# Zero products for TensorE at the heads of stages, and layer 1's head and first convolution sums moved earlier, in a four-layer graph network

## The chip, the cores and the metric

One core of a Trainium2 chip runs the whole network in one launch. The metric is device time in microseconds (us). A core has five engines, each with its own instruction queue worked in order: PE (matmuls; PEld is its weight load), DVE (vector), ACT (scalar), POOL (GpSimd, which here adds tiles and issues gathers), and SP (SyncE, which issues the other transfers). [...]

## The reference, cut

Eight batches of 2048 nodes with 64 features pass four layers; each is `x = x + layer(relu(layernorm(x)))`. `adj` is 2048x2048, sparse, and denser in its first rows.

```python
# layer 0
h = x @ W;  s = leaky_relu(h @ a_node, 0.2)
logits = where(H.T > 0, s[:, None, :], NEG)
agg = einsum('ben,bnf->bef', softmax(logits), h)          # to 64 hyperedges
industry = (adj / deg) @ (x @ W_ind)
g = ...                                                   # back to the nodes, over their hyperedges
pair = stack([industry, g]);  scores = tanh(pair @ fcW + fcb) @ av
out = einsum('bnk,bnkf->bnf', softmax(scores), pair)      # "mixing"
# layer 1: Chebyshev graph convolution, K = 3, 16 node-wise embeddings
As = [I, adj, 2 * adj @ adj - I]
x_g = einsum('knm,bmc->bnkc', As, x)
w = einsum('nd,dkio->nkio', embedding, weight)
out = einsum('bnki,nkio->bno', x_g, w) + embedding @ bias
# layer 2: three times
effects = adj @ v;  v = relu(cat(v, effects) @ W1.T + b1) @ W2.T + b2
# layer 3: attention over the edges of adj
```

## The kernel before, in words

**Tiles.** The batches are handled in four pairs q (`NP`): two batches of 64 features are the 128 partitions. Nodes are in 16 tiles of 128 (`NT`) and 4 chunks of 512 (`NC`, 4 tiles each, `TC`). "By feature" tiles have features on partitions; "by node" tiles have 128 nodes on partitions and 4x128 columns.

**Products with adj.** The adjacency is kept as lists. The first three row tiles (`HUBS`) are dense and multiplied whole; of the rest, each target tile t gets `LISTED[t]` items of 128 neighbour rows (0, 7, 6, 5, 4, ... 3; tile 0 takes 13 whole tiles). `Feed` does one such product: `dense` (L2650 on) makes 6 hub products into the bank `acc`; `listed` (L2660 on) takes item after item. For each item POOL issues a gather of 128 rows (L2613), ACT rounds it to `part_hi` (L2630), DVE subtracts to `part_lo` (L2631), and PE multiplies both by the item's 128x128 weights, cast from `cells` by ACT (L2589). Six gathers are in flight at most. Gathers read node rows from a DRAM tensor `sent`, so they wait until all 16 tiles of it are written.

**Layer 0.** `aggregate` (L896 on): per chunk the node scores (`to_pair_rows`, 4 products to 32 rows each), then per pair and chunk a broadcast of two rows of scores to 128 partitions by a product with a 32-row slice of `from_rows` (L266, L939), which DVE clips by a mask (L940). `Lists.prepare` (L2414 on) makes the lists; `x_ind` its products; `adj_product` (L310) the dense one with adj. Then `mix` (L695): for 16 (chunk, pair) steps PE makes tanh products and score products, ACT the tanh, DVE and POOL the sums; after a chunk `norm_parts` (L275), the layernorm for layer 1, is spread over the next chunk's steps. After the last chunk it runs alone: squares, a reciprocal on DVE (L291), four broadcasts and eight products on DVE (L710). The callback `each` (L881 on) gathers and turns `h` for one chunk ahead. Beside it `lists.fill` (L2507) gathers the 60 item blocks of adj and stores them as bf16.

**Layer 1** (`layer1_near`, L1640 on). Its head: `lists.load` (L2541) loads three dense row blocks through one buffer, with a DVE cast after each (L2547), and the rows for tile 0; then for 16 tiles 8 transposes of 64x64 (L1665), two copies, and a send to `sent[0]` on SP (L1667). Then the first product (16 targets, `acc` in three banks); after each target its result is sent to `sent[1]` (L1690) and turned by feature (`turn`, L1675 to 1679). Then `convolution_near`: it loads the convolution's weights and embeddings (L1708 on, L1794), makes the second product for one chunk (`product(0)`), and then walks four chunks (order 1, 0, 2, 3), in each four pairs, in each eight weight blocks taken two at a time with both batch halves, so four banks: 4 products by `w01` (128 rows), a step of the next chunk's second product, 4 products by `w2` (64 rows), and for each bank `y = (pk + bias) * emb` on DVE (L1852) and a sum on POOL (L1858) or, for the last block, on DVE.

**Layer 2** (`layer2_near`) runs three `Feed` products, then `Scores` (chunk by chunk, the layernorm for layer 3 and its score products, `pw`). **Layer 3** follows.

**What sets the order.** The program's own order fixes each engine's queue, but the framework may put independent instructions of one engine ahead of those that would wait; in the profile some of the embeddings' loads (from 639.79) and six of the first `w01` products (735.61) are ahead of their place in the text. Buffers are pools with a fixed number of tiles (`bufs`); a tile's next writer waits for the readers of the last. Every matmul goes through `mm` (L176), so groups of them are told by tile names.

## Time and profile before

| | us |
|---|---|
| median of 3 runs (lowest, highest) | 2005.93 (2004.48, 2013.83) |
| profiled execution: its own time, its span | 2004.73, 2003.0 |
| layernorm, features, checks | 0 to 103 |
| aggregation and hyperedge keys | 103 to 186 |
| lists and x_ind | 186 to 211 |
| product with adj | 211 to 449 |
| mixing | 449 to 594 |
| layer 1's head and first product | 594 to 720 |
| second product, first chunk | 720 to 765 |
| convolution | 765 to 1240 |
| layer 2 and scores | 1240 to 1700 |
| layer 3 | 1700 to 2003 |

Of 2003.0 us PE is busy 1712.0, DVE 1393.1, POOL 1036.1 and ACT 811.0. A row of the page or the timeline reads: start, time busy, engine, line, operation, the tile written and the tiles read with shape and type, how many in a row (x), and in brackets how long the engine stood idle before and what ended that. A row of windows has the stretch and its length, then for PE, PEld, DVE, ACT and POOL the busy time and the number of instructions, then the granted clock (1.00 is full), the busy share of the transfer engines and GB/s. "PEclk" on the page is the clock in tenths, 40 slices of 50 us.

### The profile page before, as it was taken

To read this page: it belongs to the slowest core of one execution; us is meant where nothing else is said; L and a number is where in the kernel's file an instruction comes from. 1 tells how busy PE (TensorE), PEld (TensorE's weight loads), DVE (VectorE), ACT (ScalarE), POOL (GpSimd) and SP (SyncE) were. 2 spreads that over 40 slices of the span, in tenths; PEclk is the share of its full clock that TensorE was granted. 3 is DMA by queue.
4 is the path that set the end of the run, shared out by engine and by line. 5 is a ranking of instruction groups with operands and counts; after the bars stand their busy time and mean duration, and the time that the engine had idled before them with its cause. 6 is when DMAs were issued, how large, how long until landed. Compare 5 with 4: busy or idle time off the path is not lost. (4 is left out here: it accounts for less than half of the span.)

```text
span 2003.0 us, 22362 instructions
## 1 busy us (share of the span) xinstructions
PE 1712.0 (85%) x7094; PEld 986.7 (49%) x7098; DVE 1393.1 (70%) x2281; ACT 811.0 (40%) x1634; POOL 1036.1 (52%) x1005
## 2 busy tenths in 40 slices
PE   6888999898977779999999998678789899378985
PEld 2446766663325544444434443567576575244432
DVE  6888788864776657676776556698787566257874
ACT  5722545445555643221110101555556553176400
POOL 1101466668734645875765453553664440657870
PEclk8888999999887979999999899889899898689997
DMA  9641223336247864232320211667687674845665
GB/s 340 260 117 44 74 95 111 106 111 202 58 135 225 242 190 123 74 116 63 85 80 32 79 48 63 214 198 253 199 261 244 184 241 136 261 117 172 172 177 193
DMA packets 125882, 305.21 MB, mean 152 GB/s; under 512 B 29345, under 2 KB 33201, under 8 KB 120241
## 3 DMA queue, kind: packets, MB, share of 16 engines
q0 software_dynamic: 45328, 149.60, 25.0%
q1 hardware_dynamic: 78112, 149.80, 22.4%
q10 hardware_dynamic: 2304, 4.20, 0.6%
q8 instruction: 60, 0.98, 0.2%
q14 instruction: 78, 0.63, 0.1%
HBM read 240.40 MB, written 63.14 MB: 152 GB/s over the span
## 5 line engine op out<-in xcount | busy, mean ns | idle before, releaser
L2613 POOL DMA_INDIRECT raw<-sent,index x300 | 315.0, 1050 | 343.0 <-DVE part_lo L2631 137.7
L2631 DVE TENSOR_TENSOR part_lo<-raw,part_hi 128x512 fp32r<-128x512 f32 x352 | 266.2, 777 | 142.9 <-ACT part_hi L2630 77.4
L2630 ACT CAST part_hi<-raw 128x512 fp32r<-128x512 f32 x352 | 212.2, 619 | 333.1 <-PE acc L176 223.5
L1858 POOL TENSOR_TENSOR half<-half,y 128x512 f32<-128x512 f32 x192 | 247.6, 1319 | 135.0 <-DVE y L1852 134.3
L176 PE MATMUL pk<-q,w 128*128 128x512 f32 (+1 forms) x768 | 301.9, 610 | 2.3 <-DVE q L1742 0.9
L176 PE MATMUL acc<-q,ident 128*128 128x512 f32 x416 | 205.9, 620 | 25.3 <-issue 12.1
L176 PE MATMUL acc<-part_hi,weights 128*128 128x512 f32 x365 | 179.3, 495 | 31.8 <-ACT part_hi L2630 17.6
L176 PE MATMUL acc<-part_lo,weights 128*128 128x512 f32 x365 | 168.6, 464 | 36.2 <-DVE part_lo L2631 27.2
L1852 DVE SCALAR_TENSOR_TENSOR y<-pk,bias,q 128x512 f32<-128x512 f32 x224 | 157.8, 743 | 55.1 <-PE pk L176 36.1
L176 PEld LDWEIGHTS pk<-q,w 128*128 128x128 f32 (+1 forms) x768 | 115.9, 190 | 156.1 <-issue 121.0
L2862 POOL DMA_INDIRECT ring<-f_rows,near x121 | 138.9, 1148 | 71.0 <-issue 30.5
L176 PEld LDWEIGHTS acc<-q,ident 128*128 128x128 f32 x416 | 77.4, 196 | 102.0 <-issue 63.2
L176 PEld LDWEIGHTS acc<-part_lo,weights 128*128 128x128 f32 x365 | 75.1, 206 | 86.9 <-DVE part_lo L2631 50.5
L176 PEld LDWEIGHTS acc<-part_hi,weights 128*128 128x128 f32 x365 | 75.0, 206 | 82.4 <-issue 48.0
L2340 POOL TENSOR_TENSOR q<-q,beta 128x512 f32<-128x512 f32 x57 | 76.1, 1337 | 71.3 <-DVE beta L2316 32.9
L176 PE MATMUL pp<-adj,x_ind_hi 128*128 128x512 f32 x256 | 90.5, 470 | 0.5 <-DVE q L864 0.3
L2933 DVE TENSOR_TENSOR q<-ring,e 128x1024 f32<-128x1024 f32 x58 | 69.9, 1218 | 20.7 <-remote 10.0
L2599 ACT CAST hub_weights<-dense 128x384 fp32r<-128x384 bf16 x80 | 40.6, 511 | 104.1 <-PE acc L176 96.9
L2340 POOL TENSOR_TENSOR q<-q,coef 128x512 f32<-128x512 f32 x57 | 63.1, 1108 | 21.2 <-DVE q L2363 16.9
L291 DVE RECIPROCAL std<-std 128x512 f32<-128x512 f32 (+1 forms) x17 | 53.7, 3161 | 27.3 <-ACT std L290 23.4
L176 PE MATMUL pp<-adj,x_ind_lo 128*128 128x512 f32 x256 | 72.0, 400 | 0.0
L2524 POOL DMA_INDIRECT listed_raw<-in_adjT_dram,cell x60 | 62.2, 1037 | 16.5 <-issue 15.8
(501 smaller groups left out, 3430.8 us busy)
## 6 DMA issues: line engine op xcount, KB each, us to landing
rows<-in_adj_dram SPq DMA_DIRECT2D x16, 1024.0 KB
adj_t<-in_adjT_dram SPq DMA_DIRECT2D x64, 256.0 KB
own<-sent SPq DMA_DIRECT2D x52, 256.0 KB
raw<-sent SPq DMA_DIRECT2D x52, 256.0 KB
sent<-u SPq DMA_DIRECT2D x48, 256.0 KB
q<-x SPq DMA_DIRECT2D x9, 1024.0 KB
links<-squares POOLq DMA_DIRECT2D x16, 512.0 KB
x<-q SPq DMA_DIRECT2D x8, 1024.0 KB
```

The lines of the kernel that those rows point to most:

```text
L176: self.nc.tensor.matmul(out, lhsT, rhs, start=start, stop=stop)
L291: nc.vector.reciprocal(std, std)
L1852: nc.vector.scalar_tensor_tensor(y, pks[b, half], bias[:, b : b + 1], emb[:, b], op0=OP.add, op1=OP.mult,)
L1858: add.tensor_add(acc, acc, y)
L2340: self.nc.gpsimd.tensor_tensor(x, x, by.unsqueeze(2).to_broadcast([P, NB, D]), op=OP.mult)
L2524: self.kern.behind(nc.gpsimd.indirect_dma_start(raw[:, i], None, rows, bass.IndirectOffsetOnAxis(ap=self.cell[:, c + i : c + i + 1], axis= ...
L2599: self.nc.scalar.copy(to, self.lists.dense[:, :, i * P : (i + 1) * P])
L2613: self.nc.gpsimd.indirect_dma_start(raw, None, self.rows[:], bass.IndirectOffsetOnAxis(ap=self.lists.index[:, c : c + 1], axis=0),)
L2630: nc.scalar.copy(hi, raw)
L2631: nc.vector.tensor_sub(lo, raw, hi.bitcast(F))
L2862: self.nc.gpsimd.indirect_dma_start(to, None, self.kern.f_rows[:], bass.IndirectOffsetOnAxis(ap=index, axis=0))
L2933: nc.vector.tensor_tensor(y.rearrange("n i (b f) -> n i b f", b=NB), block[:, i : i + 2, : NB * D].rearrange("n i (b f) -> n i b f", b=NB) ...
```

## The change

1. A helper `warm(out, n)` puts n products of zeros (128x128 bf16, columns as many as `out` has) into a bank that the next real product overwrites. It is called in `aggregate` (3 before each chunk's scores, 5 before the first broadcast), in `Lists.prepare` (4 and 4), in `each` (4 for each of the first four tiles), under the last chunk's norm in `mix` (6), before the last 8 turned half tiles (2 each), in the first product (one ahead of each listed item, accumulating zeros), in the first convolution sums (8), in layer 2's products (targets 1 and 2) and in `Scores` (8 for the two half chunks).
2. The broadcast of scores uses a 128-row weight tile `spread`, zero but for two rows, in place of the 32-row slice; the number of products is the same.
3. Layer 1's transposes, copies and sends to `sent[0]` (`turned`) go into mixing: chunk ch-1's four tiles in the steps q=2 and 3 of chunk ch, the last four after the last norm. The last chunk of mixing uses `big` in place of `end`, whose place `ah` now has.
4. `lists.fill` also loads the dense row blocks and the rows for tile 0 (16 blocks of 128x512, stored by ACT). `cells`, `dense` and `zero` hold bytes (uint8) in place of bf16. `lists.load` is gone.
5. A class `Conv` loads the convolution's weights before the first product, begins the embeddings' loads after target 8 of it, and makes the `w01` part of pair 0 in chunk 1 (`first_part`): eight of its 16 pieces after the first product, the others one by one in `product(0)`. In the chunk, pair 0 then has only its `w2` products, a DVE product in place of the multiply-add, and two more sums on POOL.
6. Layer 1 has one set of PSUM banks: 6 `pk` and 2 `acc`. Two tiles (`whole`, `o`) share memory with others.

The order of instructions on PE changes with it: in the first product the next target's hub products no longer stand among a target's items; after the last target come two hub products, the last turn, eight `w01` products, and the other hub products. On SP, weight loads of the convolution stand ahead of the last four sends to `sent[0]`.

```diff
+    def warm(self, out, n, start=True):
+        zeros = self.zeros
+        for _ in range(n):
+            self.mm(
+                out, zeros, zeros[:, :1].to_broadcast([P, out.shape[-1]]), start=start, stop=start
+            )
...
+            if q == 0:
+                self.warm(pr, heat)
...
-                    bufs[ch] = end if ch == NC - 1 else [b[:, ch % 2] for b in big]
+                    last = ch == NC - 1 and turned is None
+                    bufs[ch] = end if last else [b[:, ch % 2] for b in big]
...
+                    elif ch > 0 and turned is not None:
+                        for i in range(2):
+                            turned((ch - 1) * TC + 2 * (q - 2) + i, bank)
-                norm = self.norm_parts(ch, x, xr, sq, std, bank, write, nc.scalar)
+                norm = self.norm_parts(
+                    ch, x, xr, sq, std, bank, write, nc.scalar, 6 if ch == NC - 1 else 0
+                )
+            if turned is not None:
+                for t in range(NT - TC, NT):
+                    turned(t, bank)
...
-                    pt = bank().rearrange("f (q n) -> f q n", q=NP)
+                    pt = bank()
+                    if t < TC:
+                        self.warm(pt, 4)
+                    pt = pt.rearrange("f (q n) -> f q n", q=NP)
...
+            xe, xo = self.chebyshev(slots)
+            ah = Halves(slots, "ah", ("q4", "q5"), True)
+            def turned(t, bank):
+                s = slice(t * P, (t + 1) * P)
+                for i, (src, h) in enumerate(((xo, slice(D, P)), (xe, slice(0, D)))):
+                    pt = bank()[:, : NP * D]
+                    if t >= NT - TC:
+                        self.warm(pt, 2)
+                    pt = pt.rearrange("n (q f) -> n q f", q=NP)
+                    for q in range(NP):
+                        nc.tensor.transpose(pt[:, q], src(q)[h, s], self.ident[h, h])
+                    self.copy(columns(ah(t), i), pt)
+                nc.sync.dma_start(self.sent[0][s], ah(t))
-                self.mix(slots, ind, h_t, fcw, av, each, lambda bank: self.lists.fill(cells, w))
+                self.mix(
+                    slots, ind, h_t, fcw, av, each, lambda bank: self.lists.fill(cells, w), turned
+                )
...
+            spread = w.tile([P, NP, 2, D], F, name="spread", bufs=1)
+            for q in range(NP):
+                nc.vector.tensor_copy(
+                    spread[:, q],
+                    self.ident[:, R * q : R * q + 2].unsqueeze(2).to_broadcast([P, 2, D]),
+                )
...
+                self.warm(pl, 3)
...
-                    self.from_pair_rows(pl, q, score[:, s])
+                    if q == 0 and ch == 0:
+                        self.warm(pl, 5)
+                    self.mm(pl, spread[:, q].rearrange("p s f -> p (s f)"), score[:, s])
...
-            tc.tile_pool(reuse_waits="tile", name="cheb", bufs=2) as w,
-            tc.tile_pool(reuse_waits="tile", name="cheb_ps", bufs=2, space=PSUM) as ps,
+            tc.tile_pool(reuse_waits="tile", name="k1", bufs=1) as k,
+            tc.tile_pool(reuse_waits="tile", name="conv_ps", bufs=1, space=PSUM) as ps,
-            lists.load(w)
-            hub = Hub(w, "first_hub")
-            for t in range(NT):
-                s = slice(t * P, (t + 1) * P)
-                for i, (src, h) in enumerate(((xo, hi), (xe, lo))):
-                    pt = ps.tile([P, NP, D], F, name="pt", tag=("acc", "pz")[i], bufs=3)
+            conv = Conv(self, slots, k, ps)
+            with tc.tile_pool(reuse_waits="tile", name="cheb", bufs=2) as w:
+                hub = Hub(w, "first_hub")
+                for t in range(HUBS):
+                    hub.fill(self, t, ah(t))
+                def turn(t):
+                    s = slice(t * P, (t + 1) * P)
+                    pz = ps.tile([P, NP, P], F, name="pz", tag="pk", bufs=6)
...
-                        nc.tensor.transpose(pt[:, q], src(q)[h, s], ident[h, h])
-                    self.copy(columns(ah(t), i), pt)
-                nc.sync.dma_start(self.sent[0][s], ah(t))
-                if t < HUBS:
-                    hub.fill(self, t, ah(t))
...
-            feed = Feed(self, lists, w, self.sent[0], lambda jt: ah(jt))
-            for t in range(NT):
-                acc = ps.tile([P, CW], F, name="acc", bufs=3)
...
+                feed = Feed(
+                    self, lists, w, self.sent[0], lambda jt: ah(jt), heat=range(1, NT)
+                )
+                for t in range(NT):
+                    acc = ps.tile([P, CW], F, name="acc", bufs=2)
+                    feed.target(acc, t, hub)
...
+                    if t > 0:
+                        turn(t - 1)
+                    if t == NT // 2:
+                        conv.begin()
+                turn(NT - 1)
+                for _ in range(8):
+                    next(conv.early)
+            self.convolution_near(slots, k, ps, conv)
...
-                    )
-            for blk in range(0, NBLK, 2):
-                load_emb(0, blk)
+                next(conv.early, None)
+            for _ in conv.early:
...
-                    accs = [w.tile([P, CW], F, name="half", bufs=4) for _ in range(2)]
+                    begun = place == 0 and q < conv.EARLY
+                    if begun:
+                        accs = conv.accs[q]
+                    else:
+                        accs = [w.tile([P, CW], F, name="half", bufs=4) for _ in range(2)]
...
-                                self.mm(pk, w01[half][:, c], src(q)[:, s], stop=False)
+                                if not begun:
+                                    self.mm(pk, w01[half][:, c], src(q)[:, s], stop=False)
-                                self.mm(pks[b, half], w2[h, c], aah[h, q], start=False)
+                                if begun and half == 0:
+                                    self.warm(pks[b, half], 1)
+                                self.mm(pks[b, half], w2[h, c], aah[h, q], start=begun)
-                                y = acc if b == 0 else w.tile([P, CW], F, name="y", bufs=3)
-                                nc.vector.scalar_tensor_tensor(
-                                    y, pks[b, half], bias[:, b : b + 1], emb[:, b],
-                                    op0=OP.add, op1=OP.mult,
-                                )
-                                if b > 0:
-                                    add = nc.vector if b == NBLK - 1 else nc.gpsimd
+                                new = begun or b > 0
+                                y = w.tile([P, CW], F, name="y", bufs=3) if new else acc
+                                if begun:
+                                    nc.vector.tensor_mul(y, pks[b, half], emb[:, b])
+                                else:
+                                    nc.vector.scalar_tensor_tensor(
+                                        y, pks[b, half], bias[:, b : b + 1], emb[:, b],
+                                        op0=OP.add, op1=OP.mult,
+                                    )
+                                if new:
+                                    own = b == NBLK - 1
+                                    add = nc.vector if own else nc.gpsimd
...
+        self.cells = pool.tile([P, PLACE[NT], P], U8, name="cells")
+        self.dense = pool.tile([P, HUBS, N], U8, name="dense")
+        self.zero = pool.tile([P, FAR, P], U8, name="zero")
+        group, late, blocks, taken = 4, [], [], []
+        for h in range(HUBS):
+            for c in range(0, N, CW):
+                blocks.append((
+                    self.dense[:, h, c : c + CW], a["adjT"][h * P : (h + 1) * P, c : c + CW],
+                ))
+        zero = a["adjT"][HUBS * P :, :P].rearrange("(i p) n -> p i n", p=P)
+        for i in range(0, FAR, group):
+            n = min(group, FAR - i)
+            blocks.append((self.zero[:, i : i + n], zero[:, i : i + n]))
+        def take():
+            if blocks:
+                to, src = blocks.pop(0)
+                raw = w.tile([P, CW], F, name="block_raw", bufs=3)
+                if len(src.shape) == 3:
+                    raw = raw.rearrange("p (i n) -> p i n", n=P)[:, : src.shape[1]]
+                nc.sync.dma_start(raw, src)
+                taken.append((to, raw))
+        def store():
+            to, raw = taken.pop(0)
+            self.kern.behind(nc.scalar.copy(to, raw))
...
+            if len(taken) > 1:
+                store()
+            take()
+        while blocks:
+            take()
+            if len(taken) > 2:
+                store()
+        while taken:
+            store()
-        self.dense = pool.tile([P, HUBS, N], BF, name="dense")
-        self.zero = pool.tile([P, FAR, P], BF, name="zero")
-    def load(self, w):
-        nc, a = self.nc, self.kern.a
-        for h in range(HUBS):
-            raw = w.tile([P, N], F, name="dense_raw", bufs=1)
-            nc.sync.dma_start(raw, a["adjT"][h * P : (h + 1) * P])
-            nc.vector.tensor_copy(self.dense[:, h], raw)
-        raw = w.tile([P, FAR, P], F, name="zero_raw", bufs=1)
-        nc.sync.dma_start(
-            raw, a["adjT"][HUBS * P :, :P].rearrange("(i p) n -> p i n", p=P)
-        )
-        nc.vector.tensor_copy(self.zero, raw)
-        self, kern, lists, w, rows, kept, raws=6, casts=3, ahead=2, group=4, targets=range(NT)
+        self, kern, lists, w, rows, kept, raws=6, casts=3, ahead=2, group=4, targets=range(NT),
+        heat=(),
+        self.heat = heat
...
+                if t in self.heat:
+                    self.kern.warm(acc, 1, start=False)
...
+class Conv:
+    CHUNKS = [1, 0, 2, 3]
+    EARLY = 1
+    def __init__(self, kern, slots, k, ps):
+        self.kern, self.nc, self.k, self.ps = kern, kern.nc, k, ps
+        nc, a = self.nc, kern.a
+        self.lo, self.hi = lo, hi = slice(0, D), slice(D, P)
...
+        DO = DE * D
+        self.w01 = []
+        for i, order in enumerate(((0, 1), (1, 0))):
+            t = k.tile([P, DO], F, name=f"w01_{i}")
+            for j, kk in enumerate(order):
+                nc.sync.dma_start(t[j * D : (j + 1) * D], a["wk"][kk])
+            self.w01.append(t)
...
+    def begin(self):
+        for blk in range(0, NBLK, 2):
+            self.load_emb(0, blk)
+    def first_part(self):
+        nc = self.nc
+        s = slice(self.CHUNKS[0] * CW, (self.CHUNKS[0] + 1) * CW)
+        for q in range(self.EARLY):
+            for b in range(NBLK):
+                for half, src in enumerate(self.xs):
+                    pk = self.bank()
+                    self.kern.mm(pk, self.w01[half][:, b * P : (b + 1) * P], src(q)[:, s])
+                    acc = self.accs[q][half]
+                    y = self.k.tile([P, CW], F, name="early_y", bufs=2) if b else acc
+                    nc.vector.scalar_tensor_tensor(
+                        y, pk, self.bias[:, b : b + 1], self.emb[:, b], op0=OP.add, op1=OP.mult,
+                    )
+                    if b:
+                        nc.vector.tensor_add(acc, acc, y)
+                    yield
```

## Prediction

> **What bounds the kernel now.** I read the page first (engine shares and the 40 slices), then the table of windows by stage, then the timeline at the places where TensorE (PE) is fed late.
>
> ```profile
> PE 1712.0 (85%) x7094; PEld 986.7 (49%) x7098; DVE 1393.1 (70%) x2281; ACT 811.0 (40%) x1634; POOL 1036.1 (52%) x1005
> ...
> PEclk8888999999887979999999899889899898689997
> ```
>
> No engine is full over the whole span, and the clock granted to PE is under 9 tenths in 17 of 40 slices. So each stage has its own limit, and the windows tell it (busy time of PE, PEld, DVE, ACT, POOL, then the clock):
>
> ```profile
> 103.00:186.00 83.00, 73.82 (x371) 42.41 (x371) 67.61 (x174) 23.72 (x40) 1.57 (x21) 0.88 0.23 66
> ...
> 449.00:594.00 145.00, 122.26 (x429) 40.80 (x429) 91.32 (x121) 77.13 (x107) 97.31 (x93) 0.90 0.40 127
> 594.00:720.00 126.00, 97.43 (x436) 67.56 (x432) 85.50 (x144) 78.83 (x171) 60.95 (x60) 0.81 0.74 228
> 720.00:765.00 45.00, 32.16 (x94) 18.41 (x93) 19.24 (x30) 16.71 (x35) 17.00 (x16) 0.78 0.66 194
> 765.00:793.00 28.00, 28.00 (x94) 12.85 (x92) 23.79 (x27) 8.36 (x17) 18.14 (x13) 1.00 0.35 102
> ...
> 594.00:611.00 17.00, 10.88 (x127) 10.27 (x123) 13.60 (x26) 10.23 (x26) 0.00 (x0) 0.50 0.72 243
> ```
>
> The aggregation (103 to 186) and the body of mixing are near PE's limit. The first product (594 to 720) and the second product's first chunk (720 to 765) are not: they follow POOL's gathers and what fills the queue ahead of them. The first convolution chunk (765 on) is PE alone at full clock. The head of the first product, from the timeline:
>
> ```profile
> 589.94 3.54 DVE L710 TENSOR_TENSOR q<-q,bank 64x512 f32<-64x512 f32 x5
> ...
> 593.63 4.10 PE L1665 MATMUL pt<-ident,q 64*128 64x64 f32 x56 [2.24 <-DVE q L710]
> ...
> 603.87 9.60 SPq L1667 DMA_DIRECT2D sent<-q  x12
> ...
> 610.71 0.93 ACT L2599 CAST hub_weights<-dense 128x384 fp32r<-128x384 bf16 x2 [5.79 <-DVE dense L2547]
> ...
> 611.27 0.79 PE L176 MATMUL acc<-first_hub_h,hub_weights 128*128 128x512 f32 x1 [4.22 <-ACT hub_weights L2599]
> ...
> 617.96 1.34 POOL L2613 DMA_INDIRECT raw<-sent,index  x1 [45.76 <-DMA sent<-q]
> ```
>
> Mixing's norm ends at 593.5; then 128 transposes at half clock, 16 sends, and a load of the dense rows in three steps; the first gather comes 24.4 us after the norm. From here 60 gathers at a pitch of 1.25 us need 75 us and take 91.6 (617.96 to 709.57), 16 of it stalls. Last, two places where PE itself is slow at half clock:
>
> ```profile
> 113.38 6.63 PE L176 MATMUL pl<-cap,from_rows 32*128 32x512 f32 x8 [0.43 <-DVE logits L940]
> ...
> 735.61 7.49 PE L176 MATMUL pk<-q,w 128*128 128x512 f32 x12 [0.38 <-PE acc L176]
> ```
>
> [...] single-pass products stand 0.43 us apart at 611.87 to 616.1 and 0.23 at 617.39 on. [...] (clock 0.50 over 594 to 611 with PE busy 10.9 of 17 us, nearly all transposes). [...] the trace has 0.63 us for a bf16 and 0.62 for an f32 128x512 copy. So I put the turn of cells and dense rows to bytes at nothing.
>
> **The change, part by part** (minus is gain, us; sums are against the profiled execution, 2004.73, whose span is 2003.0 and which is 1.2 below the median 2005.93).
>
> *1. Zero products.* About 190 stand at nine places. One of 512 columns costs 0.23 at full and 0.43 at half clock (bf16, single pass; taken equal to the fp32r rows above). On the path they cost; where PE waits anyway they are free.
> - Aggregation: 3 before each chunk's scores, 5 before the first broadcast, and 128 rows in place of 32 in the 32 broadcasts. PE ran 32-row products for 9 of 10 us at 110 to 120 and was granted only 0.58, so I believe that small products don't lift the clock and 128-row ones do. From 113.38 eight took 6.63 us; DVE needs 8x0.69=5.5 for them. The saving at best is that, some 1.1, and as much at the four before: -2; 17 zero products on the path at half clock would be +7, but they stand before waits of 2 us (the pl bank waits for ACT). Range -4 to +4.
> - Lists (4+4): the x_ind products run 32 in 6.70 us at 191 to 198, 88 in 10.46 later: 2.9 to be had, DVE's low part is nearly as late: -0.5 (-2 to +1).
> - Mix head (4 for each of 4 tiles): PE idles 3.58 us at 455.45 for a gather, then the tanh products run at half clock (2 in 1.74, 10 in 5.06): 3.4 to be had. The zeros fill the idle time but their last four come between landed gathers: +0.9. Net -2.5 (-4 to +1).
> - Mix tail (6 under the 3.35 us reciprocal): the first broadcasts wait 1.97 us for PE, half of it gone: -1 (-1.5 to 0); the rest there is eight DVE products of 0.71.
> - First product (60, one per listed item): see 3. Convolution (8) and step heads of layer 2 (13 in each of 3): fed by DMA and DVE there (half-clock spells of 3 to 10 us): -1 (-6 to +3).
> - Scores tail (8 of 256 columns, twice): PE is granted 0.75 over 1680 to 1704 and is busy 20.9 of 24; the half-clock part from 1692 to 1702 is about 10 us of PE in a chain. Half would be -5; the zeros lie on that chain (8x0.21=1.7), and lift late: -2.5 (-5 to +1).
>
> *2. Layer 1's transposes move into mixing.* 12 tiles go under q=2,3 of chunks 1 to 3: 96 transposes at about 0.08 (busy 11.3 for 128) = 7.7 us, on a PE that has some 2 us of 25 free there; plus 24 copies of 0.4, half on DVE (19 of 25 busy), 12 sends on SP, and 16 copies of 0.6 on ACT and 16 loads on SP for dense and zero rows. ACT is at 18 of 25 at most, DMA at 0.7 at most; POOL's queue gets nothing new. The PE part decides: +5 (+2 to +9). It buys at the head: after the norm only 4 tiles remain, 8 x (4x0.09+2x0.21) = 6 us, the sends with them; then the landing, which took 4.5 us from the last send to 617.96. [...] First gather 11 to 13 us after the norm in place of 24.4: -12.5. The dense rows no longer gate the hub products. SP has weight loads ahead of the last four sends, a few at 0.3 to 0.5 each: +1. Taken: -11.5 (-14 to -6).
>
> *3. The first product.* PE's work at full clock: 16x6 hub products x0.23 = 22, 73 items x2x0.23 = 33.6, transposes 64x0.15 = 9.6, zeros 60x0.23 = 13.8: 79 us, against 91 for the gathers. With 3 items in a target PE needs 1.4+2.1+0.6=4.1, POOL 3.75. So zeros go under POOL if the clock is full, and buy shorter ends of stalls: 0 (-4 to +5). Embedding loads are on SP during it before as well (at 639.79), so nothing for their place. The accumulators go from 3 to 2 banks: the next target's hub products no longer slip forward; in the +5.
>
> *4. Convolution begun early.* For the first pair, 16 w01 products (0.86 each at full clock, two passes) and their 16 DVE multiply-adds (0.74) and 14 adds (0.69) leave the chunk at 765. Eight go into the time before the first gathers land (PE waits 4.65 us, POOL 11.35), which they fill: 6.9 us. The others go between gathers; six of them stood there already (the row of 735.61, holding back a hub product to 742.54). DVE has 19.2 of 45 busy there and gets 22 more. part_lo, for which gathers wait, stands behind them: 8 x 1.43 over some ten gathers, partly stall. Clock there is 0.78 and rises. Net -1 (-6 to +6). In the chunk: a pair of blocks took 7.2 us (POOL rows at 766 to 788, 5.86 busy per four adds), PE-bound; without w01 PE needs some 4.2 and POOL's 5.86 binds: four pairs in some 21 in place of 28 us: -7 (-9 to -4). The first two POOL adds are new (+2x1.3, in it).
>
> Sum: -2 -0.5 -2.5 -1 -1 -2.5 +5 -11.5 +0 -1 -7 = -24. That gives 2004.7-24=1980.7, or about 1982 beside the median.
>
> **Rivals.**
> - *Zeros don't lift the clock.* [...] The clock gains (-2 -0.5 -2.5 -1 -1 -2.5 = -9.5) go, and some 3 us of zeros lie on the path: -24+9.5+3=-11.5, so 1994.
> - *Work moved is paid where it goes.* Mixing +9 for +5, head -8 for -11.5, second product +6 for -1, chunk -4 for -7: -24+4+3.5+7+3=-6.5, so 1999. For it: mixing keeps PE 122 of 145 us busy, its last 16 idle in the main, and DVE goes to 41 of 45 in 720 to 765. Against: the clock in both is under full.
> - *Slower: zeros in PE's in-order queue.* In the first product every item's zero stands ahead of its high and low part. PE's 79 us are at full clock; before it was granted 0.81 over the stage. At a granted 0.58, 79 becomes 136 us plus the 5 of the head: some 30 more than the gathers' 91 with their own start, and the early DVE work adds 6: -24+30+7=+13, so 2019. It decides from the clock at which 79 over it passes the gathers' 91, 0.87, and eats the whole gain at some 0.69. [...]
> - *All of it:* aggregation -4, heads and tails at their best, mixing +2, second product -6: 1965.
>
> **How the numbers follow.** Forecast 1982 (1972 to 1992) 0.53; zeros without effect, 1994, 0.12; paid where it goes, 1999, 0.15; slower, 2019, 0.08; all of it, 1965, 0.12. 0.5% is 10 us, about what a measurement can tell from no change; the bounds are 1995.9 and 2016. Faster: 0.53+0.12 and two thirds of the second case, and a little of the third: 0.77. Same 0.16, slower 0.07. The range of 8 in 10 takes in the second and third case and the upper half of the best one: 1966 to 2002.
>
> **What would show it.** Right: first gather 11 to 13 us after the norm's last product; mixing's body some 5 us longer; clock over 0.9 from the first hub product on; the gathers of the first product in 88 to 92 us; chunk one's first pair in 21 us with POOL adds back to back; broadcasts at 0.23 to 0.43 us a pass in place of 0.83 a product. Wrong: rows of zero products at 0.43 with the clock still at half; gathers waiting for part_lo behind early multiply-adds; the hub product waiting for anything but the turned tiles; a wait for sent rows on POOL that is still over 20 us after the norm.

## The result, and the profile after

The changed kernel took 1998.05 us (median of 14 runs, 1986.95 to 2009.71), the kernel before beside it 2002.58 (14 runs, 1993.78 to 2013.83): ratio 0.9979, with a 95% interval of [0.9956, 1.0002] that takes in no change. So of 24 us forecast 4.5 came. The profiled execution took 1998.91, its span is 1997.2: 5.8 below the span before. First the page after:

```profile
PE 1726.5 (86%) x7260; PEld 979.7 (49%) x7284; DVE 1404.4 (70%) x2312; ACT 818.9 (41%) x1650; POOL 1045.1 (52%) x1007
...
PEclk8899999999998998999999899889899899698988
```

Slices under 9 tenths fell from 17 to 13, and PE is busy 14.5 us more. The clock rose and the time hardly fell: this is what the experiments have to explain. The windows after, for the stages shown of before (busy PE, PEld, DVE, ACT, POOL, then the granted clock):

```profile
103.00:186.00 83.00, 71.05 (x400) 43.81 (x405) 70.50 (x191) 24.07 (x43) 4.47 (x25) 0.98 0.27 78
449.00:594.00 145.00, 126.38 (x514) 44.45 (x514) 85.14 (x120) 87.22 (x134) 95.54 (x89) 0.95 0.48 159
594.00:720.00 126.00, 107.98 (x425) 62.59 (x431) 89.06 (x141) 76.29 (x162) 63.17 (x63) 0.91 0.67 199
720.00:765.00 45.00, 36.72 (x116) 21.52 (x117) 34.38 (x56) 17.79 (x35) 19.39 (x16) 0.90 0.54 176
765.00:793.00 28.00, 26.12 (x72) 9.84 (x71) 24.46 (x28) 7.44 (x15) 22.18 (x16) 0.86 0.24 75
```

The clock is up in the first four, as forecast (0.88, 0.90, 0.81, 0.78 before); in the fifth it fell from 1.00. In the fourth DVE went from 19.24 to 34.38 of 45 us, and in the fifth PE, DVE and POOL are all over 22 of 28. The head of the first product, from the timeline after:

```profile
599.80 5.70 DVE L723 TENSOR_TENSOR q<-mix,bank 64x512 f32<-64x512 f32 x8 [1.69 <-PE bank L177]
...
603.32 0.61 PE L177 MATMUL bank<-zeros 128*128 128x256 bf16 x2
...
606.36 7.38 SPq L933 DMA_DIRECT2D sent<-q  x4
...
612.82 0.79 PE L177 MATMUL acc<-first_hub_h,hub_weights 128*128 128x512 f32 x1
...
615.11 0.63 PE L177 MATMUL acc<-first_hub_l,hub_weights 128*128 128x512 f32 x1
...
616.27 0.95 POOL L2654 DMA_INDIRECT raw<-sent,index  x1 [21.84 <-DMA w1v<-in_W1T_dram]
```

(The load that the last row names was issued on SP right behind the sends.) The norm's last product ends at 605.5, the first gather is at 616.27: 10.8 us, where it was 24.5. But the norm itself ends 12 us later than before (593.5), so the first gather comes only 1.7 us earlier. Instructions cross fixed cuts, so the time is followed from event to event instead. The table holds the us between two events of a trace (first or last row of a named tile in the timeline). The runs came from several chips, and these fall into two kinds: on some (A, that of the result among them) the kernel before took 1995 to 2004 us, on others (B) 1952 to 1959; between the two traces of it some 50 of 62 us lie in layers 2 and 3. So ratios are read within one set of runs, taken beside each other on one chip, and late stages within one kind:

| from, to | before, A | after, A | forecast | before, B | head_back, B | no_early, B | back_bare_again, B |
|---|---|---|---|---|---|---|---|
| first `pl` product that isn't zeros, to first x_ind product: aggregation | 89.5 | 84.4 | -2 | 89.4 | 84.5 | 84.6 | 86.2 |
| to adj's last product | 258.9 | 262.1 | -0.5 | 258.9 | 260.3 | 260.3 | 258.6 |
| to the norm's last product: mixing | 143.7 | 158.4 | +1.5 | 141.1 | 146.9 | 151.1 | 144.4 |
| to the first gather: layer 1's head | 24.5 | 10.8 | -11.5 | 23.4 | 20.3 | 10.8 | 19.9 |
| to the second product's first gather | 103.0 | 104.6 | 0 | 98.2 | 96.5 | 101.8 | 100.2 |
| to POOL's first convolution sum | 48.5 | 46.0 | -1 | 49.1 | 45.5 | 38.9 | 38.9 |
| to the last `pk<-q,w` product | 454.2 | 458.6 | -7 | 450.8 | 454.6 | 454.1 | 454.1 |
| to layer 2's first message product | 56.9 | 58.4 | 0 | 57.1 | 61.9 | 60.7 | 58.2 |
| to the last `pw` product: layer 2, scores | 424.1 | 409.9 | -3.5 | 390.5 | 378.3 | 383.5 | 395.6 |
| to the end: layer 3 | 298.4 | 303.4 | 0 | 281.4 | 285.6 | 284.3 | 281.0 |

(Two traces of the same kernel and kind agree within 1 to 2 us up to adj's end and scatter by up to 5 in a later row. "Before, B" is one execution of 1942.83 us, below the eleven others of the kernel before on that chip, 1946.13 to 1961.21 with a median of 1951.60: its rows are some 9 us low in sum.) The changed kernel loses 14.7 in mixing where 1.5 was forecast, and 1.9 from the second product to the end of the convolution (502.7 to 504.6) where 8 were to be gained. These two are 23 us of error. Layer 2 with the scores came 14.2 shorter where 3.5 was forecast, which hides half of it, and layer 3 took 5.0 more.

### The profile page after: what moved, and what is told of

Its sections match the earlier page's. It is cut to its first block, busy times and chain, and to the rows that moved or that the text cites. A ratio compares the mean times of both kernels' runs of the same rounds, so it can differ in the third digit from the quotient of the medians.

```text
span 1997.2 us, 22775 instructions
## 1 busy us (share of the span) xinstructions
PE 1726.5 (86%) x7260; PEld 979.7 (49%) x7284; DVE 1404.4 (70%) x2312; ACT 818.9 (41%) x1650; POOL 1045.1 (52%) x1007
## 5 line engine op out<-in xcount | busy, mean ns | idle before, releaser
L177 PE MATMUL pk<-q,w 128*128 128x512 f32 (+1 forms) x768 | 307.8, 619 | 2.0 <-DVE q L1762 0.9
L1875 POOL TENSOR_TENSOR half<-half,y 128x512 f32<-128x512 f32 x180 | 230.7, 1311 | 122.2 <-DVE y L1868 121.5
L177 PE MATMUL acc<-part_hi,weights 128*128 128x512 f32 x365 | 188.8, 518 | 17.6 <-ACT part_hi L2671 10.3
L1868 DVE SCALAR_TENSOR_TENSOR y<-pk,bias,q 128x512 f32<-128x512 f32 x210 | 148.1, 743 | 57.3 <-PE pk L177 39.3
L177 PEld LDWEIGHTS acc<-part_hi,weights 128*128 128x128 f32 x365 | 74.1, 203 | 61.9 <-issue 37.6
L2640 ACT CAST hub_weights<-dense 128x384 fp32r<-128x384 uint8 x80 | 40.6, 511 | 89.4 <-PE acc L177 87.8
```

Source lines behind the costliest of these rows:

```text
L177: self.nc.tensor.matmul(out, lhsT, rhs, start=start, stop=stop)
L1868: nc.vector.scalar_tensor_tensor(y, pks[b, half], bias[:, b : b + 1], emb[:, b], op0=OP.add, op1=OP.mult,)
L1875: add.tensor_add(acc, acc, y)
L2640: self.nc.scalar.copy(to, self.lists.dense[:, :, i * P : (i + 1) * P])
```

## The experiments

**My theory** after the result: what moved is paid where it went (mixing; DVE in the second product), and the zeros lift the clock but mostly where something else ends the wait. **The rivals:** the zeros themselves are what costs (they stand ahead of other products in PE's queue); or they do nothing, since they don't raise the clock. Four sets of runs separate the parts, and a fifth goes after one point that stayed open. Each set has its own runs of the kernel before, on one chip.

### First set: the changed kernel again, and each part by itself

The kernel before took 1953.96 here. The changed kernel once more:

> The changed kernel once more, unchanged, for a second trace. If the difference of the two first traces in a stage is the change's, this trace shows it again: mixing from the last product with adj to the last norm product 158 us (before 144), layer 2 with its scores 13 us shorter than before. If it is scatter of one execution, these move by 5 us and more. Ratio to before 0.996 to 1.000.

Ratio 0.9935 [0.9913, 0.9957], 1941.59 us: a chip of kind B, and a ratio below the first 0.9979 and below what I expected: 0.2 to 0.7% is what the change is worth. Mixing is again much longer than before (154.3).

*no_zeros*, the changed kernel without any zero product:

```diff
-        for _ in range(n):
+        for _ in range(0):
```

> The changed kernel without any zero product (all else kept, the 128-row broadcast too). Theory A, the zeros lift the clock where it counts: 5 to 10 us slower than the changed kernel, the clock in the first product back from 0.91 to about 0.8, layer 2 longer by most of the 13 us. Theory B, the zeros are a wash, since they stand on the path in turned tiles (16 of 0.21, 3.4 us) and in mixing's head: within 3 us of the changed kernel or faster, first gather some 3 us sooner after the norm.

0.9920 [0.9893, 0.9948]. Beside 0.9935: all the zeros together bring nothing that this measurement can see. The aggregation took 84.5, the same as with zeros. Three windows of one place tell why; first the kernel before, then no_zeros, then the changed kernel:

```profile
110.00:120.00 10.00, 9.20 (x13) 2.79 (x14) 8.11 (x12) 2.19 (x3) 0.32 (x2) 0.58 1.05 373
```

```profile
110.00:120.00 10.00, 7.06 (x17) 2.44 (x18) 9.90 (x19) 3.60 (x4) 0.32 (x2) 1.00 1.05 373
```

```profile
110.00:120.00 10.00, 8.15 (x22) 3.17 (x23) 9.31 (x19) 3.39 (x5) 0.32 (x2) 1.00 0.95 334
```

With 32 rows PE is busy 9.20 of 10 us at a clock of 0.58; with 128 rows and no zeros it gets 1.00, and DVE (9.90 of 10) becomes the bound. So the gain of 5 is the broadcast's alone, and zeros have nothing left to give there.

Most of the rise of the clock isn't the zeros' either. In the four windows from 103 to 765 it is 0.95, 0.92, 0.88 and 0.88 without any zeros, 0.98, 0.94, 0.91 and 0.92 with them on the same chip (after_again), and was 0.88, 0.89, 0.83 and 0.82 before (B).

*zeros_only*, the kernel before with the zeros and the broadcast, without the moves. The zeros stand where they do in the change, but for those under the turned tiles and the early sums, which aren't there; `cells` hold bytes and `o` lies in `mine`, for room:

```diff
+            self.warm(pr, heat)
...
-                    self.from_pair_rows(pl, q, score[:, s])
+                    self.mm(pl, spread[:, q].rearrange("p s f -> p (s f)"), score[:, s])
```

> The kernel before with the zeros and the 128-row broadcast alone (lists in bytes and one tile's place shared, to make room). Theory A: 8 to 13 us faster than before (aggregation 5, layer 2 and scores 8). Theory B: within 4 us of before, only aggregation shorter. If mixing's head shows a stall of some 8 us with zeros here too, the zeros make it; if not, the moved work does.

0.9983 [0.9966, 1.0000]: 3.7 us in the median, and the aggregation alone is 5 shorter. Its first product has a clock of 0.88 in 594 to 720 (0.83 before, on B), so the zeros do raise it there; the stretch from norm to the second product's first gather is 124.8 us (25.5+99.3), between the 121.6 and 127.5 of two traces of before. Mixing took 142.7, as before (141.1 and 143.7): zeros without the moves don't lengthen it.

*head_back*, the changed kernel with layer 1's transposes, copies and sends back at the layer's head; loads, early sums and the zeros kept, but for the 16 zeros under the turned tiles:

```diff
-  self.lists.fill(cells, w), turned
+  self.lists.fill(cells, w), None
-                for t in range(HUBS):
-                    hub.fill(self, t, ah(t))
+                for t in range(NT):
...
+                            nc.tensor.transpose(pt[:, q], src(q)[h, s], ident[h, h])
+                        self.copy(columns(ah(t), i), pt)
+                    nc.sync.dma_start(self.sent[0][s], ah(t))
```

> The changed kernel with layer 1's transposes, copies and sends back at layer 1's head; dense rows still loaded in mixing, zeros but those of the turned tiles kept. If moving the transposes into mixing is what made it longer by 14 us, mixing returns to within 4 us of 144 and the head is some 10 us longer: the total is within 4 us of the changed kernel. If mixing stays long (its head waits for gathers and loads that stand in front), the total is 8 to 12 us slower than the changed kernel.

0.9908 [0.9885, 0.9932]: undoing the move costs nothing, its median is 5.7 below the changed kernel's (the intervals overlap). From adj's end to the second product's first gather it took 263.7, after_again 268.1, no_zeros 266.2. The move takes 20.3 to 10.8 at the head, pays 146.9 to 154.3 in mixing, and the first product is longer (96.5 to 103.0). There gathers that start earlier wait longer for a free buffer: 7.2 us for `part_hi` on ACT and 7.9 for `part_lo` on DVE in after_again, 7.0 for `part_lo` and under 1 for `part_hi` here.

### Second set: the early sums, the zeros under the turned tiles, and a best guess

The kernel before took 1951.60. The kernel before itself once more, for a second trace of it:

> The kernel before, unchanged, for a second trace beside the changed kernels of the same chip. Its stages up to the start of layer 2 lie within 2 us of the first trace (mixing from the last product with adj to the last norm product 143.7, from there to the second product's first gather 127.4). Layers 2 and 3 tell whether the zeros shorten them: theory A, they are 10 us longer here than in the changed kernel on this chip; theory B, within 4 us.

1942.83 us; its stages are the table's "before, B". For its total it is no measure, as said there.

*no_early*, the changed kernel without the early sums; the loads stay early:

```diff
-                    next(conv.early)
+                    next(conv.early, None)
-    EARLY = 1
+    EARLY = 0
```

> The changed kernel with no part of the convolution made ahead (all 16 first products of pair 0 in their old place, loads still early). If taking PE's share out of the first pair brings the 8 us forecast, this is 8 us slower. If DVE and POOL bind that pair (before, DVE was busy 23.8 of its 28 us), it is 0 to 3 us slower, or faster by what the early DVE work costs the gathers.

0.9904 [0.9880, 0.9928], 1934.0 us. The second product's first chunk is 38.9 us to POOL's first sum, where the changed kernel took 44.7, 46.0 and 43.4 in three traces; and from there on the convolution takes 454.1, no longer than with its first pair begun early (458.6, 458.7 and 454.5). Two timelines show it. The changed kernel, from the turn of the last tile on (PE, POOL and DVE):

```profile
718.40 7.03 PE L177 MATMUL pk<-q,w 128*128 128x512 f32 x16
...
724.66 0.95 POOL L2654 DMA_INDIRECT raw<-sent,index  x1 [0.30 <-issue]
...
727.29 4.45 PE L177 MATMUL pk<-q,w 128*128 128x512 f32 x10
...
729.76 0.67 DVE L2672 TENSOR_TENSOR part_lo<-raw,part_hi 128x512 fp32r<-128x512 f32 x1
...
730.70 1.76 POOL L2654 DMA_INDIRECT raw<-sent,index  x1 [5.09 <-DVE part_lo L2672]
```

and no_early:

```profile
712.18 0.95 POOL L2654 DMA_INDIRECT raw<-sent,index  x1 [10.86 <-PE acc L177]
...
713.57 1.96 PE L177 MATMUL pk<-q,w 128*128 128x512 f32 x4
...
718.55 1.16 POOL L2654 DMA_INDIRECT raw<-sent,index  x1 [1.66 <-DVE part_lo L2672]
```

This product has four buffers for gathers, so the fifth waits for one, that is for the first `part_lo`. Behind the early multiply-adds and sums on DVE it comes at 729.76, and the gather 9.8 us after the first one (720.91); without them the gather comes 6.4 after (718.55 less 712.18). PE makes the eight early products (16 passes) in one run before a hub product, where no_early's two (4 passes) stand in the gap before data lands.

*no_turn_zeros*, the changed kernel without the 16 zeros among the last turned tiles:

```diff
-                        self.warm(pt, 2)
+                        self.warm(pt, 0)
```

> The changed kernel without the 16 zeros of 256 columns ahead of the last turned tiles. They stood on PE's queue between norm and first hub product at half clock. First hub product 3.3 us after the norm in place of 7.3; the end of the first product 2 to 4 us sooner; total 0 to 4 us faster than the changed kernel. If the zeros there kept the clock up, the first product is instead 3 us longer and the total the same.

0.9905 [0.9879, 0.9931], which overlaps after_again's interval. The norm's end to the first hub product is 3.3 us, with these zeros 7.3, in every pair of traces. The row of 603.32 shown above is the first of eight: two take 0.61 between runs of transposes. The granted clock is 0.50 over 603.30 to 612.80 and over 612.80 to 615.50, that is up to the product of 615.11, and 1.00 over 615.90 to 618.00. That is 4 us paid on the path, and no_zeros starts its hub products as early as this one.

*best_a*, head_back without the zeros in aggregation, lists, mixing's head and norm:

```diff
-                self.warm(pl, 3)
...
-        kern.warm(pk, 4)
...
-        kern.warm(pb, 4)
...
-                        self.warm(pt, 4)
+                        self.warm(pt, 0)
```

> Layer 1's transposes at its own head, dense rows loaded in mixing, first convolution sums early, and zeros only in the first product, convolution, layer 2 and scores. If the zeros in aggregation, lists, mixing's head and norm do nothing (aggregation was 84.5 us with and without them), this equals the version with the transposes back: some 18 us faster than before on a chip like the second, 5 us faster than the changed kernel.

0.9940 [0.9918, 0.9962], no better than head_back (0.9908, another set), against my guess. Its aggregation took 84.6 without zeros; the rest of the difference lies within the intervals and wasn't explained.

### Third set: half of the early sums, and the parts crossed

The kernel before took 1994.96, on a chip like the first. *early_half* begins half of the 16 pieces early, the chunk makes the others:

```diff
-            for b in range(NBLK):
+            for b in range(NBLK // 2):
```

> The changed kernel with only the first eight of the sixteen early pieces, those that stand before the second product's gathers land; the others go back to the convolution. If the cost of the early part is its DVE work among the gathers' low parts, the second product's first chunk is some 5 us shorter than with all sixteen and the total 3 to 6 us faster than the changed kernel. If it is elsewhere (the zeros, the POOL sums), the total stays within 2 us.

0.9948 [0.9928, 0.9967]; the chunk took 40.3 us. Second product's first gather to the last convolution product: 495.9. The seven traces with full early sums have 497.9 to 504.6 there (mean 501.3), the nine without 487.0 to 495.9 (mean 491.3).

The other three have no early sums (`EARLY = 0`, as in no_early): *back_no_early* is head_back so, *ntz_no_early* is no_turn_zeros so, and *back_bare* is back_no_early with the `range(0)` of no_zeros as well.

> Transposes back at layer 1's head and no early convolution; dense rows and weights loaded early, zeros and 128-row broadcast kept. Both steps gave 5 to 6 us apart; if they add up, some 23 us faster than before (ratio 0.988), the fastest so far. If both came from the same place (DVE and PE around the first product), 18 us as each alone.

0.9956 [0.9934, 0.9978]; that stretch 495.9. The two steps did not add up to the 0.988 that I expected.

> The changed kernel without zeros ahead of the turned tiles and without the early convolution, transposes still in mixing. If moved transposes cost what they bring once their zeros are gone, this equals the version with them back within 3 us; some 21 us faster than before.

0.9946 [0.9928, 0.9964]; that stretch 487.0, but mixing 158.2. Beside back_no_early (0.9956) this is the move by itself, without its zeros, on one chip: 13.6 us less at the head, 8.2 more in mixing, 5.6 more in the first product, and the same time within 2.3 us.

> As the version with transposes back and no early convolution, and without any zero product. If zeros are a wash, within 3 us of it; if those in the first product and scores help (2 us each in the traces), 3 to 6 us slower.

0.9927 [0.9897, 0.9958], 1976.43: the fewest parts (the broadcast, the dense rows loaded in mixing, the weights' loads, the banks) and the lowest median of the set, 6 to 8.5 below the others; the intervals overlap.

These traces and the first one share a stall that the traces of kind B hardly show. The changed kernel, after mixing's first tanh products (PE):

```profile
455.97 1.13 PE L177 MATMUL p<-q,fcw 64*128 64x512 f32 x4
...
465.43 4.84 PE L177 MATMUL p<-q,fcw 64*128 64x512 f32 x12 [8.33 <-issue]
```

The zeros did what they were to do (four products in 1.13, two in 1.74 before), and then PE, ACT and DVE all stand until 465. First tanh product to the fifth: 9.5 there, 7.3 to 8.3 in this set's three kernels with zeros, 4.1 in back_bare on this same chip, 3.7 before. The trace says only "issue", and the transfers ran at 377 to 418 GB/s. That zeros here go with the stall is shown; what it waits for is not. In these traces most of it is made up later: from adj's end to the fifth tanh product back_no_early took 16.8 us and back_bare 10.7, but to the norm's end 150.0 and 149.5.

### Fourth set: repeats, and zeros in layer 2 alone

The kernel before took 1959.22. Changed kernel, no_early and back_bare again:

> The changed kernel, as control for the others of this call: ratio to before 0.993 to 0.999.

> The changed kernel without the early convolution. If the early part costs what the traces say (from the second product's first gather to layer 2's first product 553.7 us in place of 561.9), it is 5 to 8 us faster than the control; if that was the chip, the same within 2.

> No early convolution, transposes at layer 1's head, no zeros: what remains is the 128-row broadcast, the dense rows loaded in mixing and the weights loaded early. If the three steps taken out cost 3 to 6 us each, it is some 10 us faster than the control; if zeros gain 6 us in layer 2, only some 5.

0.9932 [0.9905, 0.9958]; 0.9899 [0.9872, 0.9926]; 0.9913 [0.9883, 0.9943]. In medians no_early_again is 8.6 us below after_third and back_bare_again 4.4. Without early sums the stretch to the convolution's end is 492.5 and 493.0, with them 497.9. *back_l2* is best_a without early sums and without the zeros in the first product, so that zeros remain only in layer 2 and the scores:

```diff
-  lambda jt: ah(jt), heat=range(1, NT)
+  lambda jt: ah(jt), heat=()
-    EARLY = 1
+    EARLY = 0
```

> As the version before it, with zeros only in layer 2's products and scores. In the traces layer 2 was 6 to 12 us shorter with zeros and layer 3 4 to 10 us longer. If the first is the zeros' and the second scatter, it is 5 us faster than the version without; if layer 3 takes it back, the same within 2.

0.9892 [0.9865, 0.9919], 1939.11: the lowest ratio of all, 6.9 below the changed kernel's median of this set; its interval overlaps the other three of the set, after_third's only just. Layer 2 and the scores took 390.1 here with zeros, 395.6, 390.5 and 388.8 without (back_bare_again, before_again, no_zeros), 378 to 386 in the others of kind B with them; on A 407 to 416 with and 417.3 and 424.1 without. But layer 3 took 283.7 to 288.8 with and 281.0 to 281.4 without on B. From the last convolution product to the end of the program that leaves, on B, 725.5 to 736.4 with zeros and 729.0 to 734.8 without: no gain that these traces show.

The end of the scores shows clearly what zeros do and why it doesn't count. The window of back_bare_again (no zeros), then of after_third:

```profile
1650.00:1655.00 5.00, 5.00 (x17) 3.22 (x17) 2.01 (x9) 0.37 (x1) 0.00 (x0) 0.50 0.16 56
```

```profile
1650.00:1655.00 5.00, 4.66 (x28) 3.57 (x28) 2.89 (x16) 1.69 (x4) 0.00 (x0) 1.00 0.41 110
```

Half clock (0.50) against full (1.00). And what layer 3's gathers wait for next, back_bare_again, then after_third:

```profile
1661.13 0.41 SPq L2969 DMA_DIRECT2D order<-order  x1
1662.99 0.15 DVE L3101 CAST own<-order 128x1 f32<-128x1 int32 x1 [0.82 <-DMA order<-order]
1663.46 0.94 POOL L2995 DMA_INDIRECT ring<-f_rows,near  x1 [24.47 <-DVE own L3101]
```

```profile
1655.76 0.43 SPq L2960 DMA_DIRECT2D order<-order  x1
1661.33 0.15 DVE L3092 CAST own<-order 128x1 f32<-128x1 int32 x1 [4.91 <-DMA order<-order]
1662.08 0.94 POOL L2986 DMA_INDIRECT ring<-f_rows,near  x1 [24.36 <-DMA x_more<-x]
```

Counted from each trace's first `pw` product (1558.5 and 1556.8), the load of the order is issued at 102.6 without zeros and at 99.0 with them, but the cast waits 4.91 in place of 0.82 for it to land, and the gather (which in the second trace waits last for a load of `x`, just behind the cast) comes at 105.0 and 105.3. The other traces of kind B agree: the gather comes at 103.7 to 105.3 without zeros and at 104.0 to 105.7 with them. From the first `pw` product to the end it is 381.8 without and 383.1 with zeros.

### Fifth set: which part of the early loads

Without early sums the second product's first chunk is 10 us shorter than before. I had put that to the loads, but the banks (six and two) changed with them. *late_emb* puts the embeddings' loads after the first product in the program, *late_loads* the weights' too (both without early sums):

```diff
-                    if t == NT // 2:
-                        conv.begin()
                 turn(NT - 1)
+                conv.begin()
```

In late_loads a line `conv.load()`, with the weights' loads out of `Conv.__init__`, stands ahead of `conv.begin()`.

> No early sums (as in the kernel without the early part), and the embeddings' loads begin only after the first product, the convolution's weights still before it. The stretch from the second product's first gather to the convolution's first POOL sum took 48 to 49 us in the kernel before and 37 to 39 in every kernel without early sums. If the early embeddings give that saving (my theory, in part), it goes back to 42 to 49; if it is the weights or the banks, it stays at 37 to 39.

0.9979 [0.9958, 1.0001]; the chunk took 36.1 us.

> As the kernel with late embeddings, and the convolution's weights are loaded after the first product too. Theory (the early loads give the saving): 46 to 50 us from the second product's first gather to the first POOL sum, as before. Rival (the six and two banks, or the gathers' own order, give it): 37 to 40. If the weights stand ahead of nothing else, the first gather of the first product comes up to 1 us earlier.

0.9938 [0.9912, 0.9964]; 38.2 us. By my own words that would be the banks. But the edit did not do what its name says. The queue of SP in late_loads, then in the kernel before:

```profile
619.06 1.87 SPq L2744 DMA_DIRECT2D w<-in_wk_dram  x3
620.98 1.23 SPq L2746 DMA_DIRECT2D w<-in_wk_dram  x2
```

```profile
715.36 0.50 SPq L1708 DMA_DIRECT2D w<-in_wk_dram  x1
...
718.57 1.77 SPq L1708 DMA_DIRECT2D w<-in_wk_dram  x3
```

The loads went ahead of their place in the text. As I read the program, that is because the framework puts a load forward to where its buffer is free: in the kernel before the weights' pool is opened after the first product's is closed, in the new kernels it is open before. The embeddings were early in all of them (639 before). So it is the weights' own place or the banks (or the order that follows from either), which no run separates. On this chip (kind A, before 2003.58) both kernels stall in mixing's head (10.5 and 9.4 us to the fifth tanh product) and mix in 162 us; whether that is why late_emb is near 1 again isn't shown.

## Why the prediction was wrong

**Right: the aggregation's direction, the head, the first product.** -5.1 for -2, outside the range given: I had counted twelve of the 32 broadcasts. That "128-row ones do" lift the clock agrees with what was measured at 110 to 120 (0.58 before, 1.00 in no_zeros); the zeros beside them add nothing. First gather 10.8 after the norm (11 to 13 forecast), -13.7 for -11.5. First product +1.6 for 0 on A (on B some 5).

**Wrong: part 2, mixing's "+5".** Mixing took 14.7 more, with the zeros' -3.5 in the forecast. The move itself costs about 8 there (158.2 and 150.0 with and without it in the third set, 154.9 and 146.9 in no_turn_zeros and head_back), within the range of "+2 to +9". What failed is that I took the 16 loads and ACT copies for the dense rows as covered, "ACT is at 18 of 25 at most, DMA at 0.7 at most", and put them at nothing: with the move and all zeros undone, mixing still takes 149.5 on A (143.7 before) and 144.4 on B (141.1 before); best_a and back_l2, which have neither there, took 148.4 and 150.4 on B. These 3 to 9 us are put to the loads and copies by elimination, since they are what is left of the change in mixing; no run takes them out alone. The zeros' -3.5 didn't come either: zeros_only mixes as before, and no_zeros (154.7) as after_again (154.3). The stall in mixing's head isn't the reason: on B, where it hardly shows, the changed kernel still loses 13.2 and 10.4 (154.3 and 151.5 for 141.1).

What the earlier gathers gain at the head is then spent in mixing and as longer waits in the first product. That is the rival "paid where it goes", with mixing still dearer than its +9 and the convolution worse than its -4. That its 1999 is within a microsecond of the result is in part luck, since layer 2's 14.2 came to its help.

**Wrong: part 4, "Net -1" and "POOL's 5.86 binds: four pairs in some 21".** Part 4 and the banks were to bring -8 up to the convolution's end; without early sums the stretch is some 10 shorter than before (491.3 against 502.7 and 500.0), and the early sums give 10 back. Two steps fail. In the second product I wrote that `part_lo` stands behind the early work "partly stall" and netted it against filled gaps; the gaps on PE were real, but the gather ring follows DVE, and the chunk is 43 to 46 us with and 36 to 40 without. In the convolution I took PE's 28.00 of 28 for the bound and POOL for the next one, 7 us below. But DVE is nearly as full as PE. The kernel before, DVE, over the first pair (from its first product to the second pair's):

```profile
767.31 1.41 DVE L1852 SCALAR_TENSOR_TENSOR half<-pk,bias,q 128x512 f32<-128x512 f32 x2 [2.66 <-PE pk L176]
...
775.74 4.42 DVE L2631 TENSOR_TENSOR part_lo<-raw,part_hi 128x512 fp32r<-128x512 f32 x3
...
784.87 2.51 DVE L2631 TENSOR_TENSOR part_lo<-raw,part_hi 128x512 fp32r<-128x512 f32 x2 [0.85 <-ACT part_hi L2630]
...
789.96 1.75 DVE L1858 TENSOR_TENSOR half<-half,y 128x512 f32<-128x512 f32 x1 [0.60 <-POOL half L1858]
...
794.09 1.40 DVE L1852 SCALAR_TENSOR_TENSOR half<-pk,bias,q 128x512 f32<-128x512 f32 x2
```

DVE is busy 24.9 of these 26.8 us, so at most 1.9 could be had before it binds, and the change adds two POOL sums. The changed kernel there (DVE and POOL):

```profile
766.16 2.78 DVE L1866 TENSOR_TENSOR y<-pk,q 128x512 f32<-128x512 f32 x4 [4.82 <-PE pk L177]
766.93 14.60 POOL L1875 TENSOR_TENSOR early<-early,y 128x512 f32<-128x512 f32 x10 [12.90 <-DVE y L1866]
...
768.86 2.82 DVE L2672 TENSOR_TENSOR part_lo<-raw,part_hi 128x512 fp32r<-128x512 f32 x2
...
774.09 0.69 DVE L1866 TENSOR_TENSOR y<-pk,q 128x512 f32<-128x512 f32 x1 [0.53 <-POOL early L1875]
...
775.88 0.57 PE L177 MATMUL acc<-part_lo,weights 128*128 128x512 f32 x1 [1.88 <-DVE part_lo L2672]
```

POOL's ten sums run back to back (14.60), as I had said they would; DVE then waits for POOL, a `part_lo` takes 1.41 in place of 0.69, and PE waits for it. The second pair's first multiply-add comes at 793.09: the pair took 26.9 us, before 26.8, so nothing of the seven came. The other six traces with full early sums have 24.6 to 30.3 for it, the twelve with none 26.8 each. The long `part_lo` is no cost of the change: the kernel before has it under POOL's sums too (775.74, three in 4.42), and that is part of why DVE was full. In the changed kernel's pair the `part_lo` under POOL's sums take 2.81 to 3.03 for two and 1.15 for the one at 778.03; the one at 785.96, half under a sum, takes 0.68, those at 791.25 and 792.45, beside none, 0.68 and 0.69. The 16 `y`, which read `pk` from PSUM, take 0.68 to 0.69 under the sums too. What makes `part_lo` longer isn't shown.

**Half right: the zeros.** They lift the clock (0.83 to 0.88 in the first product of zeros_only, 0.50 to 1.00 at the end of the scores), though less than the rest of the change does. That they would was an estimate ahead of the runs; the trace of before did not show it. The rival without effect is wrong in its reason, and the slower one didn't come up: the first product's clock was 0.91, above the 0.87 from which it was to decide. But the sum of -9.5 that I gave to the clock isn't there: 0.9920 without any zeros, 0.9935 with. The aggregation's was the broadcast's, the head's and the tail's in mixing didn't show, and the scores' was passed on to the loads ahead of layer 3. Layer 2 was shorter in most traces with zeros, but with layer 3 nothing is left of it. The turned zeros cost 4 on the path, near the 16 x 0.21 in part 2 (0.21 was an estimate for 256 columns, half of the 0.43 by which 512-column products stand apart at a clock of 0.50, 612.29 to 616.13 before), and the first product is as long with them (103.0) as without (103.5).

**Open besides:** what mixing's head waits for on A; whether the weights' place or the banks shorten the second product; what of mixing's loads costs the time; why a chip of A gives 0.9979 and two of B 0.9935 and 0.9932 for the changed kernel (the intervals overlap only just).

## What to carry to other kernels

Work that was moved out of a stall was not free here (13.6 us less at the head, 8.2 more in mixing, 5.6 more in the first product). See whether the place it goes to has room on every engine that it uses, and whether the buffers it lets run ahead are stopped by the next engine: add up DVE and POOL in the target window, not only the engine that looks full. When one engine is full in a window, see how full the next one is before pricing what is freed (here DVE was busy 24.9 of 26.8 us). A clock that rises isn't time (0.81 to 0.91 in the first product, whose time rose by 1.6): ask which wait ends the stage, and what would be late next. The parts that paid here are small and plain: a broadcast by 128 rows in place of 32 (5 us), and the weights' place or the banks in the second product (some 10 us, without early sums). back_bare and back_l2, with little more than these, are 0.7 to 1.1% faster than before (0.9927, 0.9913, 0.9892) and not slower than the whole change.

## What the hardware showed beyond expectation

- With products of zeros the granted clock at the end of the scores was 1.00 (after_third, 1650 to 1655), without them 0.50 (back_bare_again), while 32-row products busy 9.20 of 10 us were granted 0.58 (before, 110 to 120).
- DVE's `part_lo` goes from 0.69 to 1.41 us while POOL adds (the changed kernel's first pair), in the kernel before as well (1.47).
- Chips differ: the kernel before had medians from 1951.6 to 2003.6 in six sets, and in two traces the same 258.9 us from x_ind to adj's end but 424.1 and 390.5 in layer 2 and the scores.
